# A running maximum over attention scores: from single tiles in PSUM to pairs of copied tiles in SBUF

## The chip, the cores and the metric

The kernel runs on one core of a Trainium2 chip. The metric is the device time of one execution in microseconds (us), lower is better. The core has a matrix engine (TensorE, "PE" in the profile; its weight loads are listed apart as "PEld"), a vector engine (VectorE, "DVE"), a scalar engine (ScalarE, "ACT"), a general engine (GpSimd, "POOL") and a queue that issues most of the DMAs (SyncE, "SP"). Every engine works through its own instructions in a fixed order. PSUM is the memory that TensorE writes its results to; SBUF is the main on-chip memory.

## The reference

The program is a Perceiver-like stack of two layers. Each adds to the latents x (16 batches of 64 tokens, width 128) a cross attention over a context of 1601 tokens, then a state-space scan, then a feed-forward block (a mixture of experts in layer 0, a block-quantized gated one in layer 1). All is fp32. The change concerns the cross attention alone, which is in short (layer 1; layer 0 has the same form without the mask):

```python
xn = layer_norm(x, g1, b1)                  # context, 1601 tokens
ln_lat = layer_norm(latents, g2, b2)        # 64 latents
q = ln_lat @ Wq
k, v = split(concatenate([xn, ln_lat]) @ Wkv)   # 16 heads of 64
weight = einsum('bhld,bhnd->bhln', q * scale, k * scale)
weight = where(full_mask, weight, neg)
weight = softmax(weight)                    # over the 1665 keys
out = einsum('bhln,bhnd->bhld', weight, v)
return out.transpose(0, 2, 1, 3).reshape(b, l, 1024) @ Wout
```

A softmax needs, for each query, the maximum of its scores over all keys. How that maximum is built up is what changes.

## The kernel before, in words

**Tiles.** The attention is cut into 64 groups: 2 layers, 16 batches, 2 halves of 8 heads. Keys lie on the partitions, and the 8 x 64 = 512 queries of a half lie along the free dimension. The 1664 keys (1600 of the context and 64 latents; the context's last one is treated apart, in `apart_scores`) make NT = 13 tiles of 128. So a group has 13 score tiles `s` of 128 x 512 fp32, each one PSUM bank. There are three buffers for `s`.

**A score tile's way** (`scores`, lines 534 to 562). TensorE multiplies the keys by the queries into `s` (line 547; an fp32 matmul shows as two MATMUL instructions). ScalarE copies `s` to SBUF, line 554 in layer 0 and, with the key mask added as a bias, line 552 in layer 1. The copies lie in pairs: a buffer `st` of 128 x 2 x 512 holds tiles 2j and 2j+1, and the 13th tile has a buffer of its own. From tile 1 on VectorE reads the same `s` once more from PSUM and updates the running maximum `R` (128 x 512): line 561 in layer 0, and line 559 in layer 1, where the mask is added in the same instruction. That makes 12 such instructions for each group, 768 in all. A buffer of `s` is free for the tile three places on when both readers, the copy and the maximum, are done. The framework also lets no two engines read one PSUM bank together: the maximum of a tile waits for its copy.

**What follows in a group.** `maximum` (564) transposes `R` on TensorE into a PSUM tile `tm` (570), reduces it along the keys (576) and combines it with the lone last key (577 to 581). `spread` (584) lays that maximum out over the partitions again with four more transposes, `mb` (588). `weigh` (591) subtracts `mb` from a pair of copied tiles on VectorE (596) and takes the exponential on ScalarE (597), seven times for each group. `average` (599) multiplies each weighted tile by the values, four matmuls for each tile, 52 for each group (609). `gather`, `denominator`, `turn` and `output` finish the group.

**Order.** `run` (1201) goes through steps n; `step` (1318) issues in step n the scores of tile n mod 13 of group n div 13, the average of a tile from LAG = 21 steps earlier, `maximum` of the group before at its step 1, `spread` at its step 3, and a `weigh` at every second step from then on. The other work of the layers (scan, experts, feed-forward, normalizing and transposing the next contexts) consists of generators of which `run` draws a little between steps.

**The order tie.** A scheduler may move instructions, so `behind` (1301) ties the side work to the attention. `place` keeps, for TensorE, ScalarE and VectorE, the list of attention instructions issued so far: score matmuls, copies, maxima. What is traced inside `with self.behind(back)` may not come ahead of the last of them on its engine (for ScalarE and VectorE: the last but `back`). Side work is traced with `back` = 1, `maximum` and `spread` with 0.

Of the kernel before, what the change touches and what calls it, by code (L numbers as in the profile page):

```python
# [32 lines left out]
F32 = mybir.dt.float32  # L33
# [4 lines left out]
ALU = mybir.AluOpType  # L38
# [4 lines left out]
P = 128  # L43
# [9 lines left out]
NT = G + 1  # L53
NQ = 512
# [23 lines left out]
class Kernel:  # L78
# [455 lines left out]
    def scores(self, g, i):  # L534

        nc, grp = self.nc, self.groups[g]
        lay, b, half = grp["key"]
        if i == 0:
            grp["st"] = []
            grp["R"] = self.at.tile([P, NQ], F32, tag="R", name=f"R{g}", bufs=2)  # L540
        if i % 2 == 0:
            n = min(2, NT - i)
            grp["st"].append(self.at.tile([P, n, NQ], F32, tag=f"st{n}", name=f"st{g}_{i // 2}", bufs=11 if n == 2 else 2))
        st, R = grp["st"][i // 2][:, i % 2, :], grp["R"]
        q = self.q_of[lay, b][:, half * 8:half * 8 + 8, :].rearrange("p h l -> p (h l)")
        s = self.pss.tile([P, NQ], F32, tag="s", name=f"s{g}_{i}")
        mm = nc.tensor.matmul(s, self.kv_of[lay, b][1][:, i * P:(i + 1) * P], q, start=True, stop=True)  # L547
        self.place["PE"].append(mm.ins)
        masked = lay == 1
        if masked:  # L550
            mc = self.mcol[:, i, b:b + 1]
            ev = nc.scalar.activation(st, s, AF.Identity, bias=mc)  # L552
        else:
            ev = nc.scalar.copy(st, s)  # L554
        self.place["ACT"].append(ev.ins)
        if i:
            last = grp["st"][0][:, 0, :] if i == 1 else R
            if masked:
                mx = nc.vector.scalar_tensor_tensor(R, s, mc, last, ALU.add, ALU.max)  # L559
            else:  # L560
                mx = nc.vector.tensor_tensor(R, s, last, ALU.max)  # L561
            self.place["DVE"].append(mx.ins)

    def maximum(self, g):

        nc, grp = self.nc, self.groups[g]
        lay, b, half = grp["key"]
        t = self.tp(f"tm{g}")
        for k in range(4):
            nc.tensor.transpose(t[:, k * P:(k + 1) * P], grp["R"][:, k * P:(k + 1) * P], self.ident)  # L570
        m = self.sm([P, 4], "m")
        ee = self.sm([P, 4], "ee")
        se = self.se_of[lay, b][:, half * 4:half * 4 + 4]

        top, less = t[:, :4], t[:, 4:8]
        nc.vector.tensor_reduce(top, t.rearrange("p (k n) -> p k n", k=4), AX.X, ALU.max)
        nc.vector.tensor_tensor(m, top, se, ALU.max)
        df = self.sm([P, 4], "df")
        nc.vector.scalar_tensor_tensor(less, top, -1.0, se, ALU.mult, ALU.add)
        nc.vector.tensor_scalar(df, less, 0.0, None, ALU.min)  # L580
        nc.scalar.activation(ee, df, AF.Exp)
        grp["m"], grp["ee"] = m, ee
# [717 lines left out]
    @contextmanager  # L1300
    def behind(self, back=0):


        tc, block = self.tc, self.nc.cur_bb.bb
        at = len(block.instructions)
        yield
        where = {}
        for e, k in (("PE", 0), ("ACT", back), ("DVE", back)):
            if len(self.place[e]) > k:
                i = self.place[e][-1 - k]  # L1310
                where[i.engine] = i
        free = mybir.DependencyInfo(mybir.DependencyClass.NoSync, mybir.DependencyReason.DATA)
        for i in block.instructions[at:]:
            a = where.get(i.engine)
            if a is not None and a is not i:
                tc.add_manual_dep(i, a.name, free, reason="behind")
# [100 lines left out]
```

## Time and profile before

| | |
|---|---|
| median of 3 runs | 2039.4 us (2036.52 to 2041.78) |
| the profiled execution, its time | 2037.05 us |
| its span, first to last instruction | 2035.3 us |
| mean granted TensorE clock | 0.991 |
| busy: POOL, DMA engines by q1 | 512.0 us (25%), 18.1% |
| attention matmuls, busy: scores (L547), averages (L609) | 848.5 us, 866.1 us |
| maxima on VectorE, busy: L561 (two groups), L559 (two groups) | 241.6 + 22.1 us, 262.9 + 24.0 us |
| subtractions on VectorE (L596), busy | 502.5 us |
| first and last score matmul starts at | 29.9 us, 1955.9 us |

How to read the profile: each engine's busy time is the union of its instructions' times; a line of the groups names the source line, engine, operation, "written <- read" tiles, shapes and count, then the busy time and mean duration, and behind the last bar how long the engine stood idle right before these instructions, with what ended that idleness. TensorE's matmuls overlap in a pipeline, and their ends are modelled, so two that run back to back show durations longer than the distance of their starts; the distance of the starts is the pace.

### The profile page before, as it was taken

The page shows a single profiled execution, that of the slowest core. Times are in us where ns is not written, and L with a number is a line of the kernel's source. Part 1 is how long each engine was busy: PE and PEld are TensorE (multiplying, and loading weights), DVE is VectorE, ACT ScalarE, POOL GpSimd, SP SyncE. Part 2 cuts the span into 40 slices and gives each one's busy share as a digit, 9 for nine tenths or more (in the row PEclk, how much of TensorE's full clock was granted, in tenths as well). Part 3 has the DMA queues.
Part 4 walks back from the last instruction along what each step waited for, and adds up shares of the span by engine and source line. Part 5 has one row for each costly group of instructions (what it writes and reads, how often), then busy time and mean ns, then how long its engine had stood idle before and what let it go on. Part 6 is the DMA issues. An engine that isn't in the chain of part 4 may idle for free. (4 is left out here: it accounts for less than half of the span.)

```text
span 2035.3 us, 32662 instructions
## 1 busy us (share of the span) xinstructions
PE 1959.3 (96%) x12005; PEld 1486.4 (73%) x12005; DVE 1558.3 (77%) x2893; ACT 1405.2 (69%) x2673; POOL 512.0 (25%) x581
## 2 busy tenths in 40 slices
PE   7999999999999999999999999999999999999994
PEld 5677777676777766778777787777778777787783
DVE  4886667987777897776988777898686878778774
ACT  5787878888668887666767657776566656675651
POOL 3112113543113452121443203442111121101000
PEclk9999999999999999999999999999999999999996
DMA  5211112221122222221221102221120111101000
GB/s 143 69 60 52 52 52 73 82 66 50 35 76 86 66 76 57 64 74 47 67 80 50 36 24 71 75 59 51 43 56 15 57 36 47 46 1 36 23 1 21
DMA packets 142956, 110.53 MB, mean 54 GB/s; under 512 B 11458, under 2 KB 129486, under 8 KB 142798
## 3 DMA queue, kind: packets, MB, share of 16 engines
q1 hardware_dynamic: 140598, 107.40, 18.1%
q8 instruction: 95, 1.56, 0.3%
q10 hardware_dynamic: 2200, 1.06, 0.3%
q14 instruction: 63, 0.52, 0.1%
HBM read 79.97 MB, written 27.41 MB: 53 GB/s over the span
## 5 line engine op out<-in xcount | busy, mean ns | idle before, releaser
L609 PEld LDWEIGHTS av<-kv,st 128*128 128x128 f32 x6656 | 849.3, 192 | 310.1 <-issue 282.6
L609 PE MATMUL av<-kv,st 128*128 128x129 f32 x6656 | 866.1, 276 | 4.5 <-DVE aq L618 3.1
L547 PE MATMUL s<-qT,kvT 128*128 128x512 f32 x1664 | 848.5, 600 | 17.2 <-DVE R L561 14.5
L596 DVE TENSOR_TENSOR st<-st,mb 128x1024 f32<-128x1024 f32 (+1 forms) x448 | 502.5, 1135 | 1.2 <-PE mb L588 1.1
L597 ACT ACTIVATE st<-st 128x1024 f32<-128x1024 f32 (+1 forms) x448 | 445.5, 998 | 63.1 <-DVE st L596 59.5
L552 ACT ACTIVATE st<-s,mcol 128x512 f32<-128x512 f32 x416 | 283.8, 685 | 222.8 <-PE s L547 177.4
L554 ACT COPY st<-s 128x512 f32<-128x512 f32 x416 | 240.9, 583 | 125.9 <-PE s L547 99.0
L547 PEld LDWEIGHTS s<-qT,kvT 128*128 128x128 f32 x1664 | 258.9, 191 | 91.0 <-DVE R L561 40.2
L559 DVE SCALAR_TENSOR_TENSOR R<-s,mcol,R 128x512 f32<-128x512 f32 x352 | 262.9, 747 | 70.6 <-ACT st L552 69.6
L561 DVE TENSOR_TENSOR R<-s,R 128x512 f32<-128x512 f32 x352 | 241.6, 686 | 81.4 <-ACT st L554 79.6
L483 POOL TENSOR_TENSOR kv<-kv,vec 128x384 f32<-128x384 f32 (+1 forms) x128 | 135.9, 1081 | 155.4 <-PE kt L521 65.0
L628 POOL TENSOR_TENSOR aq<-aq,rd 128x512 f32<-128x512 f32 x63 | 77.0, 1222 | 359.2 <-DVE rd L625 351.9
L730 POOL TENSOR_TENSOR db<-sc_u,bb 128x512 f32<-128x512 f32 x64 | 84.8, 1327 | 134.8 <-DVE h L741 64.8
L747 POOL TENSOR_TENSOR sc_y<-sc_y,h 128x512 f32<-128x512 f32 x60 | 80.0, 1334 | 105.3 <-DVE h L746 81.3
L513 ACT ACTIVATE kv<-kv,coff,crstd 128x128 f32<-128x128 f32 x195 | 82.1, 494 | 8.2 <-POOL coff L510 8.2
L741 DVE TENSOR_TENSOR_SCAN h<-da,db 128x512 f32<-128x512 f32 x64 | 85.3, 1333 | 0.0
L504 ACT ACTIVATE scr<-kv,cmean 128x128 f32<-128x128 f32 x195 | 78.8, 404 | 6.9 <-DVE cmean L500 3.6
L561 DVE TENSOR_TENSOR R<-s,st 128x512 f32<-128x512 f32 x32 | 22.1, 690 | 78.4 <-ACT st L554 78.4
L618 DVE SCALAR_TENSOR_TENSOR aq<-xeb,ee,av 128x129 f32<-128x129 f32 x256 | 74.3, 346 | 3.4 <-PE av L609 3.4
L117 POOL TENSOR_TENSOR crstd<-cvar,neghalf 128x13 f32<-128x13 f32 x15 | 37.5, 2497 | 145.7 <-DVE cvar L508 145.5
L416 PE MATMUL q<-xnT,wqk 128*128 128x128 f32 x512 | 69.8, 281 | 0.0
L416 PEld LDWEIGHTS q<-xnT,wqk 128*128 128x128 f32 x512 | 64.4, 196 | 6.8 <-issue 3.3
(369 smaller groups left out, 1942.8 us busy)
## 6 DMA issues: line engine op xcount, KB each, us to landing
bb<-bcd SPq DMA_DIRECT2D x64, 256.0 KB, 4.4
xh<-kv SPq DMA_DIRECT2D x16, 832.0 KB, 4.8
kv<-xh SPq DMA_DIRECT2D x16, 832.0 KB, 5.4
kvT<-xhT SPq DMA_DIRECT2D x16, 800.0 KB, 4.5
xhT<-kvT SPq DMA_DIRECT2D x15, 800.0 KB, 3.5
kv<-in_ctx_dram SPq DMA_DIRECT2D x15, 768.0 KB, 5.2
ew<-in_e1T_dram SPq DMA_DIRECT2D x36, 64.0 KB, 1.8
ew<-in_e3T_dram SPq DMA_DIRECT2D x36, 64.0 KB, 1.9
```

What stands on the lines that cost most here:

```text
L416: nc.tensor.matmul(t[:, k * P:(k + 1) * P], self.wqk[:, g * 4 + k, :], xnT, start=True, stop=True)
L483: nc.gpsimd.tensor_tensor(kv[:, lo:hi, :D], kv[:, lo:hi, :D], self.row(self.vec[:, w1, :], [P, hi - lo, D]), ALU.mult)
L547: mm = nc.tensor.matmul(s, self.kv_of[lay, b][1][:, i * P:(i + 1) * P], q, start=True, stop=True)
L552: ev = nc.scalar.activation(st, s, AF.Identity, bias=mc)
L554: ev = nc.scalar.copy(st, s)
L559: mx = nc.vector.scalar_tensor_tensor(R, s, mc, last, ALU.add, ALU.max)
L561: mx = nc.vector.tensor_tensor(R, s, last, ALU.max)
L596: nc.vector.tensor_tensor(st, st, self.row(mb, [P, n, NQ]), ALU.subtract)
L597: nc.scalar.activation(st, st, AF.Exp)
L609: nc.tensor.matmul(o, st, self.kv_of[lay, b][0][:, i, :], start=(i == 0 and k % 2 == 0), stop=(i == NT - 1 and k % 2 == 1))
L730: nc.gpsimd.tensor_tensor(db, u, self.row(bb[:, 0, s % 2, :], both), ALU.mult)
L741: nc.vector.tensor_tensor_scan(flat(h), flat(da), flat(db), 0.0, ALU.mult, ALU.add)
```

## The change

The maximum is no longer taken from PSUM tile by tile. `R` becomes two tiles wide (128 x 2 x 512). Nothing happens for the tiles 0, 1 and all even ones up to 10. At tile 3 one instruction takes the elementwise maximum of the first two copied pairs, at tiles 5, 7, 9 and 11 that of `R` and the newly complete pair, each 128 x 1024 (line 562 of the changed kernel). At tile 12 one instruction folds the lone last tile into the first half of `R` (559), and one folds the second half into the first (560), each 128 x 512. `maximum` then transposes the first half. Masked and unmasked layers are treated alike, since the copies already hold the mask. VectorE's order tie counts from the last maximum in place of the last but one. Lines after the first hunk move by three: 570 becomes 573, 596 becomes 599, 609 becomes 612.

```diff
-            grp["R"] = self.at.tile([P, NQ], F32, tag="R", name=f"R{g}", bufs=2)
+            grp["R"] = self.at.tile([P, 2, NQ], F32, tag="R", name=f"R{g}", bufs=2)
...
-        if i:
-            last = grp["st"][0][:, 0, :] if i == 1 else R
-            if masked:
-                mx = nc.vector.scalar_tensor_tensor(R, s, mc, last, ALU.add, ALU.max)
-            else:
-                mx = nc.vector.tensor_tensor(R, s, last, ALU.max)
-            self.place["DVE"].append(mx.ins)
+
+        pair = grp["st"][i // 2]
+        if i == NT - 1:
+            nc.vector.tensor_tensor(R[:, 0, :], R[:, 0, :], st, ALU.max)
+            mx = nc.vector.tensor_tensor(R[:, 0, :], R[:, 0, :], R[:, 1, :], ALU.max)
+        elif i > 1 and i % 2:
+            mx = nc.vector.tensor_tensor(R, grp["st"][0] if i == 3 else R, pair, ALU.max)
+        else:
+            return
+        self.place["DVE"].append(mx.ins)
...
-            nc.tensor.transpose(t[:, k * P:(k + 1) * P], grp["R"][:, k * P:(k + 1) * P], self.ident)
+            nc.tensor.transpose(t[:, k * P:(k + 1) * P], grp["R"][:, 0, k * P:(k + 1) * P], self.ident)
...
-        for e, k in (("PE", 0), ("ACT", back), ("DVE", back)):
+        for e, k in (("PE", 0), ("ACT", back), ("DVE", 0)):
```

## The prediction, made before the changed kernel ran

> **What bounds the kernel now.** I read the busy line first, then the groups of TensorE and VectorE, the timeline of a quiet stretch, the waits of TensorE, and last the tiles that the change touches.
>
> ```profile
> PE 1959.3 (96%) x12005; PEld 1486.4 (73%) x12005; DVE 1558.3 (77%) x2893; ACT 1405.2 (69%) x2673; POOL 512.0 (25%) x581
> ...
> L547 PE MATMUL s<-qT,kvT 128*128 128x512 f32 x1664 | 848.5, 600 | 17.2 <-DVE R L561 14.5
> ...
> L559 DVE SCALAR_TENSOR_TENSOR R<-s,mcol,R 128x512 f32<-128x512 f32 x352 | 262.9, 747 | 70.6 <-ACT st L552 69.6
> L561 DVE TENSOR_TENSOR R<-s,R 128x512 f32<-128x512 f32 x352 | 241.6, 686 | 81.4 <-ACT st L554 79.6
> ```
>
> TensorE is busy 96% of the span; 2035.3 - 1959.3 = 76 us are all that it idles. VectorE is at 77%, and in front of the maxima it stands idle for ScalarE's copies. A busy row of TensorE may hide stalls, so the pace matters:
>
> ```profile
> 706.47 1.02 PE L547 MATMUL s<-qT,kvT 128*128 128x512 f32 x2
> 707.33 1.05 PE L609 MATMUL av<-kv,st 128*128 128x129 f32 x8
> 708.22 1.02 PE L547 MATMUL s<-qT,kvT 128*128 128x512 f32 x2
> 709.08 1.05 PE L609 MATMUL av<-kv,st 128*128 128x129 f32 x8
> 709.97 1.02 PE L547 MATMUL s<-qT,kvT 128*128 128x512 f32 x2
> ```
>
> The starts (first column) lie 0.86 us apart after a score pair and 0.89 after eight average matmuls: 1.75 us for a step, with nothing between. Taking for each kind of matmul the usual distance to the next start, I sum 1928 us of TensorE work over the whole trace; some 100 us remain as stalls, start and tail included. So **TensorE at its pace is the bound**. VectorE time saved is worth nothing by itself; only what makes TensorE wait for VectorE counts. The waits by who caused them:
>
> ```profile
> PE s L547 <- DVE R L561: 14.5, 17, 1.7
> ...
> PEld s L547 <- DVE R L561: 40.2, 44, 2.5
> ...
> PEld s L547 <- DVE R L559: 18.4, 28, 1.5
> ```
>
> A score matmul waits because the maximum, three tiles earlier, still holds its PSUM buffer. That is the wait that the change ends.
>
> **The change part by part.**
>
> *Removed: 768 maxima that read PSUM.* 241.6 + 22.1 + 262.9 + 24.0 = 550.6 us of VectorE. With them goes the second reader of each `s` buffer. What TensorE gets back: its idle time before scores for `R` is 14.5 us, plus 2.2 us for L559 in the waits of the second half, 16.7 us in all. The weight loads' 40.2 + 18.4 = 58.6 us is no price, since earlier matmuls still run behind most of it. Part of the stall may be hidden in stretched matmuls: the mean is 600 ns, the median 592 (tile view), so at most 8 ns x 1664 = 13 us more. Bounds 16.7 and 30 us. I take 20, near the idle row: comparing each score's start with the pace gives 20.1 us where a maximum came last. What is late next is the copy alone: over all tiles its end lies 1.7 us or more ahead of the matmul three tiles on in 95% of cases (shortest 0.78, median 4.2), against 0.06 and 3.1 us for the maximum. So no new bound follows at once.
>
> *Added: 5 pair maxima and 2 single ones for each group.* The pair form does not occur in the trace. The nearest row is the subtraction, same operation and shape but with one input in PSUM; the single one is like L561:
>
> ```profile
> L596 DVE TENSOR_TENSOR st<-st,mb 128x1024 f32<-128x1024 f32 x384 | 460.0, 1211 | 1.2 <-PE mb L588 1.1
> ```
>
> 320 x 1.21 + 128 x 0.69 = 387 + 88 = 475 us, 75 us less VectorE time than before, if nothing disturbs it. The disturbance that I expect: both inputs now lie in SBUF. The scan's two operations of that kind run beside a busy POOL, and the maxima that read PSUM do too:
>
> ```profile
> L741 DVE TENSOR_TENSOR_SCAN h<-da,db x64: 1196/1218/2294, 350.6 to 1379.0; 128x512 f32<-128x512 f32 x64
> L746 DVE TENSOR_TENSOR h<-h,bb x60: 665/683/1792, 360.3 to 1383.1; 128x512 f32<-128x512 f32 x60
> ...
> L561 DVE TENSOR_TENSOR R<-s,R x352: 624/689/702, 34.0 to 991.2; 128x512 f32<-128x512 f32 x176
> ```
>
> (Shortest, median, longest in ns.) SBUF-only operations stretch up to 2.6 times; those with an input in PSUM never do. Means are 1333 and 765 ns, 115 and 82 over their medians; beside a POOL instruction the medians are 1416 and 826. I take 0.1 us for each new maximum, 448 x 0.1 = 45 us, bounds 0 and 448 x 0.2 = 90 us. VectorE then saves 75 - 45 = 30 us, bounds +75 and -15. On the path it costs nothing by itself; TensorE's work covers it.
>
> [...] If every new maximum met a POOL instruction of the trace's usual 1.04 to 1.3 us whole, VectorE would end up far busier than before; by the rows, a quarter to a half of them meet one for a part.
>
> [...]
>
> *Lengthened: the end of each group.* `tm` waits for the last maximum. Before, that is copy, then one maximum; now copy, a maximum, and a second one that needs the first: +0.69 us, and about 0.1 for the dependence. The trace never shows `tm` waiting for `R` by more than a trifle. Pairing the 64 last maxima with the first weight load of `tm`, the margin is 0.15 us at least, 0.66 at the 5th percentile, 1.22 at the 10th, 3.1 in the median. A uniform shift by 0.8 us would stall four or five groups for about 0.4 us, 2 us. But the built program also sets other VectorE work between these maxima. By the order of the instructions with the trace's durations, TensorE has 5.3 us of work from the 13th score to `tm` in the tight groups (6.2 median, both kernels); VectorE's work from the last pair maximum to the end of the last one is 2.4 us in the median (1.9 before), 4.3 at the 90th percentile (2.85), 6.0 at most (4.2). In 14 groups 3.3 us or more of it stands against at most 5.7 us of TensorE; before, in 2. Tile 11's copy ends some 0.9 us ahead of tile 12's, which ends 1.2 us after its matmul's start; with 1.21 us for the pair, the queue restarts at about 1.5 us. So a group stalls by 1.5 + work - 5.3: 2.2, 1.1, 0.9, 0.5, 0.5 and, against 6.2, 0.5 us, together 5.7. I take 6 us; bounds 0 (the work was done earlier) and 15 x 1.5 = 22 us (each of the 15 groups, lengthened by a collision). Behind `tm` in TensorE's queue stand scores and averages; everything shifts.
>
> *Moved: the order tie.* Side work of VectorE now stands behind a pair maximum that waits for the current copy, not the one before: at odd steps about a step, 1.75 us, later, at even steps as before. What hides it: TensorE's own queue of attention work. Uncovered, the rows of waits on side work (`me`, `gu`, `gr`: 1.6, 0.7, 1.1 us) would grow; 1 us, inside the error. No DMA is added or removed; POOL and SP have the same instructions, and POOL's collisions (L628 `aq`, 1222 ns on average) meet no waiting TensorE row above 0.6 us.
>
> *The tail.* The last group's maximum ends at 1957.27 + 0.75 = 1958.02, `tm`'s weight load starts at 1959.35: 1.3 us of margin cover 0.8. Nothing.
>
> **Sum**, against the profiled execution's own 2037.05 us (span 2035.3 and 1.75 around it): 2037.05 - 20 + 6 = 2023. That execution is 2.35 us under the median of the runs, 2039.4; against the median I forecast **2025 us**, 0.7% faster.
>
> **The rivals.** The measurement can tell 0.3% from no change, that is 6 us: faster is below 2033.3, slower above 2045.5.
>
> 1. *Forecast, 0.62.* The buffers come free earlier, `tm` costs little: 2012 to 2033.
> 2. *The gain is given back, 0.20.* The change does what it says, but TensorE, no longer held at the scores, arrives sooner at `tm`, `mb` and the averages, whose operands come through the same VectorE queue: 2039.4 - 16.7 + 15 = 2038. For: median margins of 3 us are of the size of single waits. Against: the averages' rows show only 4.5 us of idle.
> 3. *Slower, 0.12: the last maximum.* At `tm` TensorE waits for the two dependent maxima, stretched by POOL. At 1 us in half of the groups, 32 us: 2039.4 - 20 + 32 = 2051. It decides once the stalls at `tm` pass 26 us, 0.41 us for each group. For: the 14 tight groups, the collisions. Against: the median margin of 3.1 us.
> 4. *More than forecast, 0.06.* The stretched matmuls were all stalls and `tm` costs nothing: 2039.4 - 30 = 2009. Of the 100 us of stalls, start and tail keep most.
>
> The range 2008 to 2046 takes in the bounds (2039.4 - 30 = 2009 and 2039.4 - 16.7 + 22 = 2045) and all but the slower rival. Faster 0.62 + 0.06 = 0.68, same 0.20, slower 0.12.
>
> **What would show it.** Right: no TensorE wait of scores for `R`; L562 at a mean of 1.25 to 1.35 us with a longest above 1.8; VectorE busy 1520 to 1540 us; waits of `R` for copies well under the present 158.0 + 122.1 us; `tm` with a new wait for `R` of about 6 us; TensorE's busy time near 1950 us in a shorter span. Wrong: waits for L560 at `tm` above 20 us; scores that wait for the copies instead (ScalarE held up by late subtractions); or TensorE's stall staying near 100 us under other names.

## The result and the profile after

The changed kernel takes 2094.89 us (median of 4 runs, 2093.2 to 2096.88); the kernel before, beside it, 2040.59 us (4 runs). The ratio is **1.026, interval 1.024 to 1.028: 54 us slower**. The profiled execution took 2093.2 us, its span is 2091.2, the mean granted TensorE clock 0.982 (before 0.991).

The page of the changed kernel, busy line and TensorE's two attention rows (after the last bar: idle time before these instructions, and what ended most of it):

```profile
PE 1978.0 (95%) x12005; PEld 1503.3 (72%) x12005; DVE 1567.6 (75%) x2573; ACT 1403.7 (67%) x2673; POOL 584.1 (28%) x581
...
L612 PE MATMUL av<-kv,st 128*128 128x129 f32 x6656 | 868.5, 277 | 15.1 <-DVE aq L621 14.5
L547 PE MATMUL s<-qT,kvT 128*128 128x512 f32 x1664 | 849.6, 604 | 13.9 <-ACT st L554 10.8
```

The work of TensorE is the same, 12005 matmuls. The scores no longer wait for a maximum, as forecast; they now wait for copies, and the averages for the gather (`aq`), which cost 3.1 us before:

```profile
L609 PE MATMUL av<-kv,st 128*128 128x129 f32 x6656 | 866.1, 276 | 4.5 <-DVE aq L618 3.1
```

VectorE has 320 instructions fewer and is busy 9 us longer. POOL has the same 581 instructions and is busy 72 us longer. The waits of TensorE on which the rest of the text rests (total, times, longest, in us):

```profile
PE tm L573 <- DVE R L560: 15.3, 11, 2.9
PE av L612 <- DVE aq L621: 14.5, 13, 2.3
PE s L547 <- ACT st L554: 10.8, 7, 3.9
...
PE tm L573 <- DVE cmean L500: 5.4, 2, 3.7
...
PE s L547 <- ACT st L552: 3.1, 5, 1.0
```

The two waits put down to `cmean` are waits for `R` as well: L500 is the instruction right behind L560 on VectorE (692.59 in the timeline below), and the 2257 VectorE instructions that count up a semaphore in this trace all count up the same one, for which `tm` waits. So `tm` waits 20.7 us for the maximum, where it did not before. The new maxima, by the view of the tile R (shortest, median and longest in ns):

```profile
L562 DVE TENSOR_TENSOR R<-R,st x256: 1185/1219/2241, 37.2 to 2010.5; 128x1024 f32<-128x1024 f32 x128
...
L562 DVE TENSOR_TENSOR R<-st,st x64: 1209/1226/1833, 35.3 to 1992.9; 128x1024 f32<-128x1024 f32 x64
L559 DVE TENSOR_TENSOR R<-R,st x64: 658/693/1753, 54.6 to 2013.2; 128x512 f32<-128x512 f32 x64
L560 DVE TENSOR_TENSOR R<-R x64: 624/692/1329, 55.3 to 2013.9; 128x512 f32<-128x512 f32 x64
```

The medians are the undisturbed 1.22 and 0.69 us, the longest nearly twice that and more. Laid beside POOL's records, all 63 maxima that are over 0.2 us too long ran while one of POOL's four large tensor operations (`kv`, `aq`, `db`, `sc_y`) ran: 63 of the 130 that met one for over 0.05 us, none of the 318 others. POOL's own operations are longer too, `sc_y` for one, first in the kernel before and then in the changed one:

```profile
L747 POOL TENSOR_TENSOR sc_y<-sc_y,h 128x512 f32<-128x512 f32 x60 | 80.0, 1334 | 105.3 <-DVE h L746 81.3
```

```profile
L750 POOL TENSOR_TENSOR sc_y<-sc_y,h 128x512 f32<-128x512 f32 x60 | 99.0, 1651 | 121.8 <-DVE h L749 71.7
```

One stall of 3.7 us, in the timeline (start and duration in us; in brackets the idle time before and what ended it):

```profile
684.42 1.27 POOL L750 TENSOR_TENSOR sc_y<-sc_y,h 128x512 f32<-128x512 f32 x1
684.55 2.22 DVE L562 TENSOR_TENSOR R<-R,st 128x1024 f32<-128x1024 f32 x1
...
686.69 1.21 DVE L599 TENSOR_TENSOR st<-st,mb 128x1024 f32<-128x1024 f32 x1
...
687.94 1.06 ACT L600 ACTIVATE st<-st 128x1024 f32<-128x1024 f32 x1 [3.00 <-DVE st L599]
...
689.12 1.27 POOL L733 TENSOR_TENSOR db<-sc_u,bb 128x512 f32<-128x512 f32 x1 [3.43 <-DVE h L744]
689.47 1.06 ACT L554 COPY st<-s 128x512 f32<-128x512 f32 x2
689.80 1.13 DVE L559 TENSOR_TENSOR R<-R,st 128x512 f32<-128x512 f32 x1
690.86 1.21 DVE L599 TENSOR_TENSOR st<-st,mb 128x1024 f32<-128x1024 f32 x1
691.99 0.68 DVE L560 TENSOR_TENSOR R<-R 128x512 f32<-128x512 f32 x1
...
692.59 0.16 DVE L500 TENSOR_SCALAR cmean<-cmean 128x13 f32<-128x13 f32 x1
...
692.81 1.09 PE L573 MATMUL tm<-ident,R 128*128 128x128 f32 x4 [3.66 <-DVE cmean L500]
```

It is to be read from the top. A pair maximum starts 0.13 us after a POOL sum that reads SBUF, and takes 2.22 us in place of 1.22: about as much longer as the POOL sum still runs (684.42 + 1.27 - 684.55 = 1.14). The subtraction behind it comes a microsecond late, ScalarE stands 3.00 us before the exponential, and two score copies queue behind that. The 13th tile's maximum meets the next POOL operation and takes 1.13 in place of 0.69 us, again by about what was left of it. Another subtraction stands between it and the fold, and `tm` comes 3.66 us late.

After this stall TensorE's clock is lower for a while. The same place by stretches (bounds and length in us, busy times with instruction counts, then the granted clock, the DMA share and GB/s):

```profile
660.00:692.00 32.00, 28.59 (x172) 20.74 (x170) 30.56 (x43) 21.66 (x39) 15.88 (x16) 1.00 0.31 95
692.00:700.00 8.00, 7.19 (x33) 6.18 (x34) 4.12 (x10) 6.47 (x22) 2.53 (x2) 0.57 0.01 2
700.00:732.00 32.00, 32.00 (x207) 24.95 (x206) 24.70 (x31) 27.15 (x63) 18.03 (x13) 1.00 0.26 79
```

A clock of 0.57 over 8 us is half speed (a granted 0.50, from 692.05 to 698.87) for 6.8 of them. By the trace's clock records the changed kernel ran at half speed for 41 us between 30 us and its last score, in ten stretches of 3.4 or 6.8 us; the kernel before for 3.4 us, in one.

I put both together by the distances of all matmul starts, against the usual distance for each kind: what exceeds it by over 0.15 us at full clock is a *stall*, what exceeds it inside a half-clock stretch is *clock*.

| profiled execution | stalls, us | clock, us | span, us |
|---|---|---|---|
| before | 50.5 | 7.3 | 2035.3 |
| after | 86.6 | 24.2 | 2091.2 |

36 + 17 = 53 of the 56 us between the spans. The table takes in the start and the tail, where both kernels have stalls and half speed as well; it is the differences that count.

### The profile page after: what moved, and what is told of

Same layout as the page of the kernel before. It is cut to its first block, busy times and chain, and to the rows that moved or that the text cites. A ratio compares the mean times of both kernels' runs of the same rounds, so it can differ in the third digit from the quotient of the medians.

```text
span 2091.2 us, 31865 instructions
## 1 busy us (share of the span) xinstructions
PE 1978.0 (95%) x12005; PEld 1503.3 (72%) x12005; DVE 1567.6 (75%) x2573; ACT 1403.7 (67%) x2673; POOL 584.1 (28%) x581
## 5 line engine op out<-in xcount | busy, mean ns | idle before, releaser
L547 PE MATMUL s<-qT,kvT 128*128 128x512 f32 x1664 | 849.6, 604 | 13.9 <-ACT st L554 10.8
L562 DVE TENSOR_TENSOR R<-R,st 128x1024 f32<-128x1024 f32 x256 | 335.0, 1309 | 67.9 <-ACT st L554 48.9
L547 PEld LDWEIGHTS s<-qT,kvT 128*128 128x128 f32 x1664 | 265.3, 193 | 86.2 <-issue 45.0
L483 POOL TENSOR_TENSOR kv<-kv,vec 128x384 f32<-128x384 f32 (+1 forms) x128 | 152.7, 1211 | 170.1 <-PE kt L521 68.5
L631 POOL TENSOR_TENSOR aq<-aq,rd 128x512 f32<-128x512 f32 x63 | 87.3, 1386 | 295.8 <-DVE rd L628 292.8
L562 DVE TENSOR_TENSOR R<-st,st 128x1024 f32<-128x1024 f32 x64 | 81.2, 1268 | 115.4 <-ACT st L554 60.4
L733 POOL TENSOR_TENSOR db<-sc_u,bb 128x512 f32<-128x512 f32 x64 | 94.6, 1481 | 146.2 <-DVE h L744 75.8
L750 POOL TENSOR_TENSOR sc_y<-sc_y,h 128x512 f32<-128x512 f32 x60 | 99.0, 1651 | 121.8 <-DVE h L749 71.7
L579 DVE TENSOR_REDUCE tm<-tm 128x4 f32<-128x512 f32 x64 | 44.4, 693 | 80.5 <-PE tm L573 80.5
L559 DVE TENSOR_TENSOR R<-R,st 128x512 f32<-128x512 f32 x64 | 52.2, 816 | 28.1 <-ACT st L554 13.9
```

The lines of the kernel that those rows point to most:

```text
L483: nc.gpsimd.tensor_tensor(kv[:, lo:hi, :D], kv[:, lo:hi, :D], self.row(self.vec[:, w1, :], [P, hi - lo, D]), ALU.mult)
L562: mx = nc.vector.tensor_tensor(R, grp["st"][0] if i == 3 else R, pair, ALU.max)
L631: eng.tensor_tensor(aq[:, :, :D], aq[:, :, :D], self.bc(rd, [P, 4, D]), ALU.mult)
L733: nc.gpsimd.tensor_tensor(db, u, self.row(bb[:, 0, s % 2, :], both), ALU.mult)
L750: nc.gpsimd.tensor_tensor(y, y, h, ALU.add)
```

## The experiments

Two theories went in. **C, contention:** the new maxima have both inputs in SBUF, block POOL's SBUF readers and are blocked by them, and the lateness reaches TensorE. **Q, queue:** not the durations but the order costs, namely the doubled end of the maximum and the new order tie. Times are medians; ratios are to the kernel before on the same chip, with their intervals.

| kernel | time, us | ratio |
|---|---|---|
| e1: before, maxima read the copies | 2093.64 | 1.025 (1.023 to 1.027) |
| e2: after, tie undone | 2101.54 | 1.029 (1.027 to 1.031) |
| e3: before, new tie | 2059.99 | 1.008 (1.006 to 1.010) |
| e4: after, fold ahead of the last tile | 2082.53 | 1.020 (1.017 to 1.022) |
| e5: before, quiet POOL (control) | 2029.77 | 0.995 (0.993 to 0.996) |
| e6: after, quiet POOL | 2039.49 | 0.999 (0.998 to 1.001) |
| e7: e1, quiet POOL | 2032.57 | 0.995 (0.993 to 0.997) |
| e8: before, four s and two tp buffers | 2050.0 | 1.005 (1.003 to 1.006) |
| e9: e1, two tp buffers (control) | 2124.67 | 1.042 (1.039 to 1.045) |
| e10: e9, R in PSUM | 2065.62 | 1.012 (1.009 to 1.014) |
| e11: before, two tp buffers | 2070.54 | 1.014 (1.011 to 1.016) |
| e12: e4, quiet POOL | 2032.89 | 0.995 (0.994 to 0.997) |

**e1, only the operand moved** (and, in layer 1, the mask's addition dropped, since the copy holds the mask).

```diff
-            if masked:
-                mx = nc.vector.scalar_tensor_tensor(R, s, mc, last, ALU.add, ALU.max)
-            else:
-                mx = nc.vector.tensor_tensor(R, s, last, ALU.max)
+            mx = nc.vector.tensor_tensor(R, last, st, ALU.max)
```

> The kernel before, with one edit: the twelve single-tile maxima of a group stay where they are, but read the copy st in SBUF in place of the PSUM tile s (in layer 1 without adding the mask again). No pairs, no fold at the end, order tie as before. Theory C (contention: maxima with both inputs in SBUF block and are blocked by POOL): VectorE's maxima stretch as in the changed kernel, POOL's operations too, and the time rises to 2060 to 2100 us. Theory Q (queue: the late and doubled end of the group's maximum, and the new order tie, are what costs): the PSUM buffers come free early, nothing else changes, 2020 to 2035 us.

Measured: 2093.64 us, 52 us lost of the changed kernel's 54, with no pair, no fold and the old tie. So the operand's place alone can make the loss. That it is POOL which the maxima then collide with, e7 and e10 show below.

**e2 and e3, the order tie.** One constant, `("DVE", 0)` or `("DVE", back)`, either way.

> The changed kernel with VectorE's order tie as before (the last but `back` maximum). If the tie is what makes VectorE's side work late (a part of Q), most of the 54 us come back: 2040 to 2060 us. Theory C, and Q by the doubled end alone: within 12 us of the changed kernel's 2095 us.

> The kernel before, with only the new order tie (side work of VectorE behind the last maximum, not the last but one). If the tie costs: over 2055 us. Theory C: 2035 to 2050 us, no change that matters.

Measured: undone in the changed kernel, the tie brings nothing back (1.029 against 1.026; the intervals overlap). Put alone into the kernel before it costs 18 us, outside C's 2035 to 2050 and as expected only if the tie itself costs: its profiled execution, with a span 26 us longer than that of the kernel before, has 56.8 us of stalls and 24.3 of clock (before 50.5 and 7.3), so 17 of the 26 us are half-clock time. The tie is no free edit, but it isn't what made the changed kernel slow.

**e4, the doubled end.** The fold of the halves moves from tile 12 to tile 11:

```diff
         if i == NT - 1:
-            nc.vector.tensor_tensor(R[:, 0, :], R[:, 0, :], st, ALU.max)
-            mx = nc.vector.tensor_tensor(R[:, 0, :], R[:, 0, :], R[:, 1, :], ALU.max)
+            mx = nc.vector.tensor_tensor(R[:, 0, :], R[:, 0, :], st, ALU.max)
         elif i > 1 and i % 2:
             mx = nc.vector.tensor_tensor(R, grp["st"][0] if i == 3 else R, pair, ALU.max)
+            if i == NT - 2:
+                mx = nc.vector.tensor_tensor(R[:, 0, :], R[:, 0, :], R[:, 1, :], ALU.max)
```

> The changed kernel with the fold of the two halves of R right after the pair maximum of tile 11, ahead of the last tile's maximum, so that one maximum and not two stand between the last copy and tm. Theory Q: the 23 us of new waits at tm go, and with them a part of the half-clock windows: 2050 to 2072 us. Theory C: the chain is still made of stretched operations behind a stretched queue; under 20 us come back, 2075 to 2095 us.

Measured: 2082.53 us, 12 us back: within C's range, not Q's. `tm` still waits 15.4 us (waits of TensorE):

```profile
PE tm L574 <- DVE R L559: 11.2, 9, 2.1
...
PE tm L574 <- DVE cmean L500: 4.2, 2, 2.5
```

So with a single maximum at the end `tm` still comes late. With POOL quiet as well (e12 below) `tm` waits 0.5 us for it, so the lateness is that of the disturbed queue.

**e5, e6, e7, POOL made quiet.** The four large POOL operations become memsets of their outputs, which write SBUF and read nothing there:

```diff
-            nc.gpsimd.tensor_tensor(kv[:, lo:hi, :D], kv[:, lo:hi, :D], self.row(self.vec[:, w1, :], [P, hi - lo, D]), ALU.mult)
+            nc.gpsimd.memset(kv[:, lo:hi, :D], 0.5)
...
-        eng.tensor_tensor(aq[:, :, :D], aq[:, :, :D], self.bc(rd, [P, 4, D]), ALU.mult)
+        if eng is nc.gpsimd:
+            eng.memset(aq[:, :, :D], 0.5)
+        else:
+            eng.tensor_tensor(aq[:, :, :D], aq[:, :, :D], self.bc(rd, [P, 4, D]), ALU.mult)
...
-                nc.gpsimd.tensor_tensor(db, u, self.row(bb[:, 0, s % 2, :], both), ALU.mult)
+                nc.gpsimd.memset(db, 0.01)
...
-                    nc.gpsimd.tensor_tensor(y, y, h, ALU.add)
+                    nc.gpsimd.memset(y, 0.01)
```

> Control: the kernel before, with POOL's four large products and sums (kv by the norm weights, aq by 1/denominator, db, sc_y) replaced by memsets of the same outputs. That part of the computation is left out (values are constants), so that POOL hardly reads SBUF. Both theories: the maxima read PSUM, so little changes on TensorE's path: 2015 to 2045 us.

> The changed kernel with the same four POOL operations replaced by memsets (that part of the computation left out). Theory C (contention): the maxima return to their undisturbed 1.22 and 0.69 us, and the time falls to within 15 us of its control, at best below it. Theory Q (order and doubled end, whatever the durations): still 30 to 55 us above its control.

> The kernel before with single-tile maxima reading the SBUF copies, and the same four POOL operations replaced by memsets (that part of the computation left out). Theory C: at or below its control, since only the early release of the PSUM buffers is left: -20 to +8 us. If the loss came from another order or from the PSUM wait's absence: still 40 us or more above its control.

Measured: the changed kernel's loss shrinks from 54 to 2039.49 - 2029.77 = 9.7 us, that of e1 from 52 to 2.8 us, which the intervals don't tell from nothing. The control is itself 12 us faster than the kernel before (2041.54 us beside it), so each is held against the control. The tile R in e6:

```profile
L562 DVE TENSOR_TENSOR R<-R,st x256: 1191/1219/1270, 36.9 to 1959.0; 128x1024 f32<-128x1024 f32 x128
...
L559 DVE TENSOR_TENSOR R<-R,st x64: 660/692/694, 57.9 to 1961.7; 128x512 f32<-128x512 f32 x64
L560 DVE TENSOR_TENSOR R<-R x64: 623/691/694, 58.6 to 1962.4; 128x512 f32<-128x512 f32 x64
```

Medians as before, and the long ones are gone: 1270 in place of 2241 ns. A quiet POOL is also a shorter one (`aq` takes 532 ns in e6 in place of 1386), so fewer maxima meet it; but 62 of them met one of these memsets in e6, and the longest of these took 1227 ns. Still, e7 is no faster than its control, though its score buffers come free early. The waits of TensorE in the control e5 and then in e7:

```profile
PE s L547 <- DVE R L561: 8.0, 11, 1.1
...
PE av L609 <- DVE aq L618: 3.1, 3, 2.3
```

```profile
PE av L606 <- DVE aq L615: 10.9, 13, 2.3
...
PE s L547 <- ACT st L554: 3.5, 4, 1.8
```

The wait for R goes, the gather's grows by 7.8 us and the copies' by 3.5: TensorE meets the next thing that VectorE and ScalarE are late with.

**e12**, the early fold with quiet POOL:

> The changed kernel with the fold ahead of the last tile, and POOL's four large operations replaced by memsets (that part of the computation left out). Without contention only the order of the maxima differs from the quiet control at 2029.8 us. If the doubled end explains the 9.7 us that the changed kernel keeps above it: 2025 to 2033 us. If the pairs as such do (TensorE meets later subtractions and gathers): 2035 to 2042 us.

Measured: 2032.89 us, 6.6 of the remaining 9.7 us, so without contention most of the rest goes with the doubled end. The waits at `tm` are just 1.6 us in e6 and 0.5 in e12; where the other 5.5 us arise isn't shown.

**e8, e9, e10, e11, R in PSUM.** A quiet POOL leaves work out; the same question with all of it. A bank is freed by giving the small transposes two buffers in place of three (the pool tp, `pst`). In e10 the running maximum lies in that bank:

```diff
+        self.psr = pool("psr", 1, space=PSUM)
...
+            grp["Rp"] = self.psr.tile([P, NQ], F32, tag="Rp", name=f"Rp{g}")
...
-            last = grp["st"][0][:, 0, :] if i == 1 else R
-            mx = nc.vector.tensor_tensor(R, last, st, ALU.max)
+            last = grp["st"][0][:, 0, :] if i == 1 else grp["Rp"]
+            mx = nc.vector.tensor_tensor(R if i == NT - 1 else grp["Rp"], last, st, ALU.max)
```

> Control for the next: the kernel before with single-tile maxima reading the SBUF copies (R in SBUF), and two in place of three PSUM buffers for the small transposes, so that one bank is free. Both theories: what the copied maxima cost (about 51 us) plus what the third buffer is worth: 2090 to 2125 us.

> As the control, but the running maximum lies in the freed PSUM bank until the 13th tile, whose maximum writes it to SBUF: each maximum but a group's first and none other has just one input in SBUF. All of the computation is there, the tiles, the order tie and the release of the score buffers are the control's. Theory C (contention through two SBUF inputs): the maxima return to 0.68 to 0.70 us and 30 to 50 us come back, 2045 to 2075 us. Theory Q (order, early release, lateness as such): within 12 us of the control.

> The kernel before (maxima from PSUM) with two in place of three PSUM buffers for the small transposes: the price of that buffer alone. Theory C: 2045 to 2065 us, within 15 us of the kernel with R in PSUM, and 35 to 55 us under the control with copied maxima.

Measured: 2124.67 with R in SBUF, 2065.62 with R in PSUM: **59 us from where R lies**. e10 stands 4.9 us under e11, whose maxima read the scores from PSUM; their intervals overlap, so that difference is not clear of the noise. e11 itself, 2070.54 us, came 5.5 us above the range given for it. The stalls are 104.5 us in e9 and 52.4 in e10. In e9 the maxima with R in SBUF are stretched as in e1 (up to 1811 ns in both):

```profile
L558 DVE TENSOR_TENSOR R<-R,st x704: 622/686/1811, 37.0 to 2038.8; 128x512 f32<-128x512 f32 x176
```

The view of the tile Rp in e10 has both kinds side by side:

```profile
L560 DVE TENSOR_TENSOR Rp<-Rp,st x640: 665/692/771, 38.4 to 1974.7; 128x512 f32<-128x512 f32 x160
L560 DVE TENSOR_TENSOR Rp<-st x64: 681/700/1620, 37.6 to 1949.8; 128x512 f32<-128x512 f32 x64
L560 DVE TENSOR_TENSOR R<-Rp,st x64: 659/687/692, 58.7 to 1976.7; 128x512 f32<-128x512 f32 x64
```

704 maxima with one input in SBUF never exceed 771 ns, though 176 of them met one of POOL's large operations in the same way; the 64 with both there reach 1620. R is written as well as read, so e10 moves an output too; but those 64 write PSUM and are stretched all the same, and `R<-Rp,st` writes SBUF and isn't. It is the inputs that count.

> The kernel before with four PSUM buffers for s and two in place of three for the small transposes: the wait of the scores for the maximum is taken away by a buffer, with the maxima as they were. If the 20 us of that wait are to be had at all: 2018 to 2030 us, unless the two transpose buffers make waits of their own (then 2035 to 2060, with waits at the tiles of that pool). If TensorE merely meets the next wait: 2033 to 2045 us.

Measured: 2050.0 us, in the range of the third case, two transpose buffers with waits of their own (e11 shows that these cost 28 us by themselves); the rows of such waits are small, 2.3 us at `at` and 1.9 at `mb`. Against e11, which differs in the fourth score buffer alone, e8 is 20.5 us faster. So the wait for R can be worth 20 us, part of it clock: up to its last score e11 ran 20 us at half speed, e8 3.4. Yet the early release was worth 4.9 us in e10, within the noise, and nothing in e7. What decides between these stays open.

## Why the prediction was wrong

**The bound**: right. TensorE's matmuls and pace are the same; 53 of the 56 us between the spans are time in which it waits or runs at half clock.

**The wait for R, -20 us**: it ended as forecast, 16.7 us of idle time to none. The gain did not stay: 13.9 us of waits for copies and 11.4 us more for the gather took its place, as in the second rival. Even with POOL quiet e7 gained nothing. "No new bound follows at once" rested on the copies' margins of the kernel before, 1.7 us or more in 95% of cases. In the changed kernel the same margin is 0.67 us at the 5th percentile and 0.05 at its shortest (median 4.2, as before).

**The new maxima**: well sized on VectorE. Forecast 475 + 45 = 520 us; measured 335.0 + 81.2 + 52.2 + 49.6 = 518.0, the pairs at 1268 and 1309 ns. VectorE's busy time did not fall for that: instructions that follow each other overlap by some 0.08 us in the records, and 320 fewer of them overlap less: 1908 times, 153.9 us in all, before 2197 times, 188.5 us (e6 has 72 us less of maxima than e5 and is busy 44 us less).

**The step that failed** is the one after it: "On the path it costs nothing by itself; TensorE's work covers it." It put the stretched maxima at nothing on TensorE's path; with POOL quiet 44.6 of the 54.3 us go, so that is their price there, the clock and most of the waits at `tm` included (the prices in this section overlap and don't add up). The reading that a quarter to a half of the maxima meet POOL held, 130 of 448, and so did the mean. But a mean of 0.1 us for an instruction is not 0.1 us everywhere: it is 0.6 us on average in one of seven (63 of the 448 are over 0.2 us too long), spread over 39 of the 64 groups, in a fixed queue, against margins at `tm` that were 1.2 us or less in one group of ten. And I dismissed POOL's side because no TensorE row above 0.6 us waits for it; POOL's `aq` went from 1222 to 1386 ns and its `sc_y` from 1334 to 1651, and VectorE's own `h` from 765 to 915.

That operations with both inputs in SBUF stretch beside a busy POOL stood in the prediction, with the right direction, and was weighed as busy time alone. The runs now show both what it costs and when it is absent: 59 us from R in SBUF rather than in PSUM (e9 against e10), and no stretch of the pairs beside a POOL operation that only writes SBUF (e6: 1227 ns at most for a pair beside a memset).

**`tm`, +6 us**: mis-sized. It waited 20.7 us, near the upper bound of 22. Of the total, the doubled end is worth 12.4 us (e4), 6.6 with POOL quiet (e12).

**The order tie, 1 us**: not confirmed. Alone it costs the kernel before 18 us (e3), in the changed kernel nothing (e2).

**The clock**: no step of mine had it; 17 us. Of the ten half-clock stretches here, of 3.4 or 6.8 us, nine began in or at most 1.5 us after stalls of 2.3 to 4.1 us (the distance of two starts beyond the pace), and the tenth had no stall of 1 us before it; the one in the kernel before followed two gaps of 0.98 and 0.76 us. The length of a stall alone does not tell them: stalls of 2.7 us, one in each kernel, had no half-clock stretch after them.

The signs named for being wrong all came: 20.7 us at `tm`, scores that wait for copies (13.9 us), stalls of 87 us under other names. The third rival was the right sign and place, `tm` late through stretched maxima, but at 2051 us too small: it priced `tm` alone, and neither the gather and the copies nor the clock.

## What to carry to other kernels

Before an operand moves from PSUM to SBUF, look whether the instruction then has two SBUF inputs beside a busy POOL; if one of them can stay in PSUM, leave it there (59 us here, e9 against e10). Price such a collision by its longest cases against the margins of whoever waits for the queue, not by its mean against the engine's busy time. A wait that is removed is a gain only after the next wait in the same queue has been looked up, and where TensorE is the bound, time at half speed can come on top of a stall: here nine of ten half-clock stretches, of 3.4 or 6.8 us, came after stalls of 2.3 to 4.1 us.

## What the runs showed of the hardware that was not expected

- A VectorE maximum of two SBUF inputs (128 x 1024) took up to 2241 ns in place of 1219 beside POOL's tensor operations, and 1227 at most beside memsets of the same outputs.
- Half-clock stretches came in steps of 3.4 us, nine of ten after stalls of 2.3 us and more; they made 17 of the 56 us between the spans here, and 17 of the 26 us of the order tie alone (e3).
- Taking one PSUM buffer of three from the small transposes cost 28 us (e11).
